# Last convolution of a four-layer network: swapped weight columns for every second row pair, stores of two rows in one run, whole images loaded

## Chip, cores and metric

The kernel runs on one core of one Trainium2 chip, in float32. The metric is device time in microseconds (us) of the whole program, from launch to the last output landed; lower is better. Times of several runs are given as their median. Besides these there is one execution taken by the hardware profiler, from which every duration below comes.

## What is computed

The input x has 8 images of 16 channels with 256 x 256 pixels. Four residual layers follow one another, each of the form x = x + f(group norm of x): a 3x3 convolution with capsule routing, a 3x3 convolution over B-spline and SiLU features, an attention over 16x16 patches, and last a convolution. Only the last one matters here. The reference writes it with Fourier transforms:

```python
def _L3_conv_ref(x, weight):
    B, Ci, H, W = x.shape
    k, p = (K_SIZE, PAD)
    w_pad = _circular_pad(weight, H, W, k, p)
    dL = jnp.asarray(np.outer(_diag_L(H, k), _diag_L(W, k)))
    Lw = jnp.fft.fft2(w_pad * dL)
    Kx = jnp.fft.ifft2(x, norm='ortho')
    z = jnp.einsum('oihw,bihw->bohw', Lw, Kx)
    y = jnp.fft.fft2(z, norm='ortho')
    return jnp.real(y).astype(x.dtype)
...
x = x + _L3_conv_ref(_gn(x), L3_conv_weight)
```

A product of Fourier transforms is a circular convolution, and the mask dL keeps all nine taps of the 3x3 kernel. So each output pixel is a sum over 16 channels and 3x3 neighbours, where rows and columns wrap around at the image's edges, plus the pixel itself (the residual). The group norm has 8 groups of two channels: it is a scale and a shift per image and group.

## The kernel before

The program runs the layers in turn (net_kernel, L1608). Layers 0, 1 and 2 keep their results in HBM scratch; layer 0's order of work comes from a planner with due times, layers 1 and 2 are loops written out by hand. Their code is not touched, except that layer 2 fetches the first image of layer 3 and that two constants grow.

How the last layer's input lies. Layer 2 (attend, L1402) makes one channel of one image at a time and stores it to self.x3[b], a scratch of [8, 16, 16, 2, 258] (r, c, h, k, w). With g = 2h + k, the entry (r, c, g) is image row 8g + r of channel c, with one wrapped pixel added on each side. Read with (r c) as partition, an image is a [128, 32 x 258] tile: partition (r, c) holds 32 rows, eight apart. The first 32 partitions need a 33rd row, the image's first, for the wrap.

The convolution as matmuls. Four blocks of 32 partitions hold two image rows (r = 2k, 2k + 1) of 16 channels each. A matmul contracts one such block (K = 32) with a 32 x 32 weight block, whose columns are (output channel, ro), ro being one of two output rows; its moving operand is two rows g, g + 1 of 256 pixels, so N = 512. An output row pair needs four input rows, that is two blocks (q = 0, 1), and three column shifts dw: 6 matmuls. products (L1519) runs for one s (a quarter image), one q: 3 shifts x 4 row pairs j x 4 column groups c, 48 matmuls. [...] Output row 1 + 8g + 2j + ro of channel o ends in PSUM partition 32c + 2o + ro, at j and g. In before, g = 8s + 2c, so that a quarter s covers 64 rows and the four column groups 16 rows each.

The scale of the norm is multiplied into the weights, and the identity of the residual is added (weights, L1507, one VectorE instruction of 192 columns per image); the shift becomes a bias that the eviction adds.

Eviction and stores. finish (L1535) evicts the two PSUM tiles of a quarter with two instructions of 128 x 1024 into y3, a [128, 2, 4, 256] tile with five buffers: even quarters on ScalarE (L1545), odd ones on VectorE (L1543). Then SP stores it with eight DMAs (L1553), one per column group c and per ro. A partition holds rows of one parity, so each row of 256 pixels is a run of 1 KB by itself, 16 channels x 8 rows per DMA, 128 KB; row 256 wraps to row 0 with a DMA of its own. An image takes 33 of them.

Loads. The tile pt[0] of layer 2 (early2, L1291) is free while the last image runs; there first3 (L1390) loads 24 of the 32 rows of image 0 on SP's queue, when channel 6 is reached. The other 9 rows (x3r) and a copy of rows 23 to 25 (x3e[...]) come at the start of layer 3, on SP. All other images come in halves of 17 (or 16 + 1) rows, tile x3s with five buffers, on POOL's queue (fetch, L1497): five halves are asked for at once, then one more at each half as a buffer comes free, which is when TensorE has read the half that was in it.

The order within layer 3 is that of the code (tc.manual_schedule, L1578): per image b and half (s = 0 and 2), four PSUM tiles[...]; q = 0 for both quarters, each followed by two small copies ("seen", L1594); then q = 1 for both, each followed by finish. The statistics of the last image's norm ("g3b") run as small steps between the halves. [...]

The constants and weights that grow: ident3 is part of a constant block loaded after layer 0 (net_kernel, L1612; constants, L302), w3 is loaded in early3 (L1303).

Of the kernel before, what the change touches and what calls it, by code (L numbers as in the profile page):

```python
# [10 lines left out]
F32 = mybir.dt.float32  # L11
# [7 lines left out]
P = 128  # L19
WP = W + 2  # L20
# [86 lines left out]
def _ident3():  # L107

    a = np.zeros((4, 2, C, 3, 2, C, 2), np.float32)
    for c in range(C):  # L110
        for ro in range(2):
            a[:, 1 - ro, c, 1, ro, c, ro] = 1.0
    return a.reshape(P, 3 * 2 * 32)
# [16 lines left out]
def _layout(w0, bw, sw, sc, bias, wq, bq, wk, bk, wv, bv, w3):  # L130
# [37 lines left out]
    l3 = l3.reshape(P, 3 * 2 * 32)  # L168
# [110 lines left out]
class _Net:  # L279
# [950 lines left out]
    def stats3_steps(self, pool, name, bank):  # L1230
# [31 lines left out]
        def sums():  # L1262

            for q in range(4):
                at = slice(32 * q, 32 * q + 32)
                for k in range(6):
                    nc.tensor.matmul(
                        z()[at, :8], self.w3[at, k // 2, k % 2], nm[at], start=k == 0, stop=k == 5
                    )
# [21 lines left out]
    def early2(self, pool):  # L1291

        self.w2 = {
            name: pool.tile(shape, F32, name=f"w2_{name}")
            for name, shape in dict(qk=[P, 2, 512], v=[P, 2, 256], bqk=[P, 512], b2v=[P, 2]).items()
        }
        self.pt = [pool.tile([P, 2, C, 8, 32], F32, name="pt0")]
        self.emb0 = pool.tile([P, 2, 256], F32, name="emb0")
        self.mv2 = pool.tile([P, 2, 8], F32, name="mv2")
        self.nc.vector.memset(self.mv2, 0.0)  # L1300
        self.small = pool

    def early3(self, pool):  # L1303

        self.st3 = pool.tile([P, P, 6], F32, name="st3"), pool.tile([P, 2, P], F32, name="mv3")
        self.nc.vector.memset(self.st3[1], 0.0)
        self.w3 = pool.tile([P, 3, 2, 32], F32, name="w3")
        self.nc.sync.dma_start(out=self.w3.rearrange("p d t m -> p (d t m)"), in_=self.d["l3"])
        self.small = pool
# [80 lines left out]
    def first3(self, b):  # L1390

        xs = self.pt[0].rearrange("p h c r f -> p (h c r f)")[:, : 24 * WP].rearrange("p (g w) -> p g w", w=WP)
        self.fetch3(b, 0, 24, xs)
        self.x3s = xs
# [67 lines left out]
    def fetch3(self, b, g, n, xs):  # L1462

        rows = self.x3[b].rearrange("r c h k w -> (r c) (h k w)")
        at = xs.rearrange("p g w -> p (g w)")
        for k in range(g, g + n, 8):
            m = min(8, g + n - k)
            if k < 32:
                self.nc.sync.dma_start(
                    out=at[:, (k - g) * WP : (k - g + m) * WP], in_=rows[:, k * WP : (k + m) * WP]  # L1470
                )
            else:
                self.nc.sync.dma_start(out=at[0:32, (k - g) * WP : (k - g + 1) * WP], in_=rows[0:32, 0:WP])

    def layer3(self, images=range(B)):
# [6 lines left out]
        with ExitStack() as st:  # L1482
# [14 lines left out]
            def fetch(n):  # L1497
                xs = io.tile([P, 17, WP], F32, name="x3s", bufs=5)
                rows = self.x3[images[n // 2]].rearrange("r c h k w -> (r c) (h k) w")
                if n % 2:  # L1500
                    nc.gpsimd.dma_start(out=xs[:, :16], in_=rows[:, 16:])
                    nc.gpsimd.dma_start(out=xs[:32, 16], in_=rows[:32, 0])
                else:
                    nc.gpsimd.dma_start(out=xs, in_=rows[:, :17])
                return lambda k, g: xs[32 * k : 32 * k + 32, g - n % 2 * 16 : g - n % 2 * 16 + 2]

            def weights(b):  # L1507
                ws = io.tile([P, 3, 2, 32], F32, name="ws3")
                nc.vector.scalar_tensor_tensor(
                    ws.rearrange("p d t m -> p (d t m)"),  # L1510
                    self.w3.rearrange("p d t m -> p (d t m)"),
                    stat[b][0][:, 1, b : b + 1],
                    self.k["ident3"],
                    ALU.mult,
                    ALU.add,
                )
                return ws

            def products(s, q, ws, xs, ps):  # L1519

                for dw in range(3):
                    for j in range(4):
                        k = (j + q) % 4
                        for c in range(4):
                            g = 8 * s + 2 * c + (j + q) // 4
                            nc.tensor.matmul(  # L1526
                                ps[j // 2][32 * c : 32 * c + 32, j % 2].rearrange("p (g w) -> p g w", w=W),
                                ws[32 * k : 32 * k + 32, dw, q],
                                xs(k, g)[:, :, dw : dw + W],
# [5 lines left out]
            def finish(b, s, ps):  # L1535

                y = io.tile([P, 2, 4, W], F32, name="y3", bufs=5)
                bias = stat[b][1][:, b : b + 1]
                for k in range(2):
                    src = ps[k].rearrange("p j (g w) -> p g j w", w=W)  # L1540
                    to = y[:, :, 2 * k : 2 * k + 2]
                    if s % 2:
                        nc.vector.tensor_scalar(to, src, bias, None, ALU.add)  # L1543
                    else:
                        nc.scalar.activation(to, src, AF.Identity, bias=bias)  # L1545
                for c in range(4):
                    for ro in range(2):
                        row = 64 * s + 16 * c + 1 + ro
                        n = 8 if row + 14 < H else 7
                        yc = y[32 * c : 32 * c + 32].rearrange("(o r) g j w -> r o (g j) w", r=2)[ro]  # L1550
                        for first, m, at in ((0, n, row),) if n == 8 else ((0, 7, row), (7, 1, 0)):
                            to = self.out[b, 0, at]
                            nc.sync.dma_start(  # L1553
                                out=bass.AP(tensor=to.tensor, offset=to.offset, ap=[[H * W, C], [2 * W, m], [1, W]]),
                                in_=yc[:, first : first + m],
                            )

            images = list(images)
            rest = io.tile([P, 9, WP], F32, name="x3r", bufs=1)
            self.fetch3(images[0], 24, 9, rest)  # L1560
            edge = io.tile([P, 3, WP], F32, name="x3e", bufs=1)
            nc.sync.dma_start(
                out=edge, in_=self.x3[images[0]].rearrange("r c h k w -> (r c) (h k) w")[:, 23:26]
            )

            def first(k, g):
                part = slice(32 * k, 32 * k + 32)
                if g + 2 <= 24:
                    return self.x3s[part, g : g + 2]
                return edge[part, g - 23 : g - 21] if g == 23 else rest[part, g - 24 : g - 22]  # L1570

            seen = [io.tile([P, 2, 2], F32, name=f"seen{k}", bufs=1) for k in range(2)]
            halves = 2 * len(images)
            xs = {0: first, 1: first}
# [3 lines left out]
            with tc.manual_schedule():  # L1578
                for n in range(2, min(7, halves)):
                    xs[n] = fetch(n)  # L1580
                for n, b in enumerate(images):
                    for s in (0, 2):
                        i = 2 * n + s // 2
                        if 7 <= i + 4 < halves:
                            xs[i + 4] = fetch(i + 4)
                        ps = [[psum.tile([P, 2, 512], F32, name="p3") for _ in range(2)] for _ in range(2)]
                        for q in range(2):
                            for k in range(2):
                                products(s + k, q, ws, xs[i], ps[k])
                                if q:  # L1590
                                    finish(b, s + k, ps[k])
                                else:
                                    for h in range(2):
                                        (nc.vector.tensor_copy if k else nc.scalar.copy)(  # L1594
                                            seen[k][:, h], ps[k][h][:, :, 0]
                                        )
                        if todo:
                            todo.pop(0)[2]()
# [75 lines left out]
```

## Time and profile before

| what | value |
|---|---|
| median of 3 runs | 6721.79 us (6716.23 to 6725.06) |
| profiled execution, its time | 6718.79 us |
| profiled execution, its span | 6716.9 us |
| layer 3, first to last matmul | 6447.4 to 6697.9 us, 250.5 us |
| from the last eviction's end (6700.2) to the span's end | 16.7 us |
| stores issued at L1553 | 264 |
| TensorE busy over the whole span | 91% |
| mean granted TensorE clock | 0.985 |

The span is the time from the first to the last instruction of the profiled execution; its own time is 1.9 us longer, and lies 3.0 us below the median. Engines: PE is TensorE, PEld its weight load, DVE VectorE, ACT ScalarE, POOL GpSimd, SP the queue that issues most DMAs. DMA queue q1 holds what SP issues, q0 what POOL issues, q8 the instruction blocks. A float32 matmul appears as two instructions. "Issue" as a releaser means that the engine waited for nothing that the profile shows.

Layer 3 is 3.7% of the span. The rest, layers 0 to 2, is the same code in both kernels.

### The profile page before, as it was taken

To read this page: it belongs to the slowest core of one execution; us is meant where nothing else is said; L and a number is where in the kernel's file an instruction comes from. 1 tells how busy PE (TensorE), PEld (TensorE's weight loads), DVE (VectorE), ACT (ScalarE), POOL (GpSimd) and SP (SyncE) were. 2 spreads that over 40 slices of the span, in tenths; PEclk is the share of its full clock that TensorE was granted. 3 is DMA by queue.
4 is the path that set the end of the run, shared out by engine and by line. 5 is a ranking of instruction groups with operands and counts; after the bars stand their busy time and mean duration, and the time that the engine had idled before them with its cause. 6 is when DMAs were issued, how large, how long until landed. Compare 5 with 4: busy or idle time off the path is not lost. (4 is left out here: it accounts for less than half of the span.)

```text
span 6716.9 us, 111531 instructions
## 1 busy us (share of the span) xinstructions
PE 6114.0 (91%) x46024; PEld 2774.9 (41%) x46024; DVE 5400.4 (80%) x6374; ACT 2737.3 (41%) x3898; POOL 3230.2 (48%) x2098
## 2 busy tenths in 40 slices
PE   3899899899989999898897799999999999999998
PEld 1333333333333333333333344444444466666655
DVE  5799999999999999999998899999999633333321
ACT  1333333333333333333332688888888421111211
POOL 0566666666666666666667444434334211111100
PEclk9999999999999999999998899999999999999999
DMA  6233333333333333333332555555556633334257
GB/s 260 61 87 90 92 91 93 90 88 91 91 90 91 89 88 88 88 88 88 88 88 61 171 176 177 176 176 178 176 175 177 178 86 87 80 93 106 74 190 220
DMA packets 392784, 801.99 MB, mean 119 GB/s; under 512 B 57282, under 2 KB 222178, under 8 KB 354770
## 3 DMA queue, kind: packets, MB, share of 16 engines
q1 hardware_dynamic: 356242, 730.29, 37.7%
q10 hardware_dynamic: 33792, 33.82, 1.5%
q0 software_dynamic: 2240, 30.75, 1.2%
q8 instruction: 361, 5.91, 0.4%
q14 instruction: 149, 1.22, 0.1%
HBM read 584.00 MB, written 210.77 MB: 118 GB/s over the span
## 5 line engine op out<-in xcount | busy, mean ns | idle before, releaser
L745 POOL TENSOR_TENSOR dd<-dd 128x1024 f32<-128x1024 f32 x512 | 1214.0, 2371 | 617.1 <-DVE dd L736 597.1
L1001 PE MATMUL ps<-bases,tw 128*32 128x512 f32 (+1 forms) x13824 | 1361.4, 546 | 17.1 <-POOL bases L970 7.0
L736 DVE SCALAR_TENSOR_TENSOR dd<-rb,v 128x1024 f32<-128x1024 f32 (+1 forms) x1024 | 1066.9, 1083 | 99.0 <-PE rb L725 92.5
L970 POOL TENSOR_TENSOR bases<-e,a 128x1024 f32<-128x1024 f32 (+1 forms) x264 | 621.4, 2376 | 929.0 <-DVE e L968 928.7
L624 DVE TENSOR_TENSOR pr<-v,fb 128x2048 f32<-128x2048 f32 (+1 forms) x512 | 1011.6, 2017 | 24.1 <-PE pl L634 12.7
L518 PE MATMUL cv<-kt,w 128*128 128x512 f32 x2048 | 999.4, 610 | 27.9 <-DVE dd L736 21.5
L527 ACT COPY v<-cv 128x1024 f32<-128x1024 f32 x512 | 517.1, 1010 | 1152.9 <-PE cv L522 1152.9
L1001 PEld LDWEIGHTS ps<-bases,tw 128*32 128x32 f32 x13824 | 594.4, 109 | 805.6 <-issue 485.4
L745 POOL TENSOR_TENSOR s<-s,dd 128x512 f32<-128x512 f32 x512 | 670.8, 1310 | 35.0
L725 PE MATMUL rb<-rs,ct_fold 32*128 32x512 f32 x3584 | 610.2, 651 | 71.4 <-ACT rs L707 67.9
L745 POOL TENSOR_TENSOR s<-v,dd 128x512 f32<-128x512 f32 x256 | 330.7, 1292 | 660.2 <-DVE dd L736 660.2
L634 PE MATMUL pl<-pr,ct_fold 128*32 128x512 f32 x3584 | 534.3, 608 | 120.1 <-DVE pr L624 120.1
L522 PE MATMUL cv<-kt,w 64*128 64x512 f32 x2048 | 578.7, 641 | 0.0
L518 PEld LDWEIGHTS cv<-kt,w 128*128 128x128 f32 x2048 | 353.7, 190 | 524.0 <-issue 298.9
L1426 ACT ACTIVATE vt<-pv,w_b2v 128x128 f32<-128x128 f32 x512 | 146.2, 368 | 842.4 <-PE pv L1422 842.4
L1415 PE MATMUL pqk<-w_qk,t 128*128 128x512 f32 x1024 | 482.7, 594 | 4.6 <-POOL t L1409 4.6
L1447 DVE TENSOR_TENSOR y<-po,res 128x512 f32<-128x512 f32 x128 | 88.5, 691 | 487.3 <-PE po L1442 487.3
L978 DVE SCALAR_TENSOR_TENSOR bases<-xr,xm,bases 128x1024 f32<-128x1024 f32 (+1 forms) x264 | 447.6, 1734 | 0.3 <-POOL bases L970 0.3
L1409 POOL TENSOR_TENSOR t<-t,emb 128x512 f32<-128x512 f32 x128 | 162.3, 1268 | 511.0 <-DVE t L1405 500.3
L955 ACT ACTIVATE sq<-a 128x1024 f32<-128x1024 f32 (+1 forms) x264 | 263.8, 999 | 229.5 <-DVE a L947 228.7
L725 PEld LDWEIGHTS rb<-rs,ct_fold 32*128 32x128 f32 x3584 | 173.3, 186 | 416.4 <-issue 221.1
L937 ACT ACTIVATE d<-xr,bd,sd 128x1024 f32<-128x1024 f32 (+1 forms) x264 | 319.0, 1208 | 15.8 <-DMA xr<-x1p 15.8
(264 smaller groups left out, 8386.1 us busy)
## 6 DMA issues: line engine op xcount, KB each, us to landing
kt<-d SPq DMA_DIRECT2D x256, 516.0 KB
xr<-x1p SPq DMA_DIRECT2D x120, 1024.0 KB
d<-dn ACTq DMA_DIRECT2D x64, 516.0 KB
x<-y SPq DMA_DIRECT2D x128, 258.0 KB
xs<-in_x_dram SPq DMA_DIRECT2D x16, 2048.0 KB
xs<-in_x_dram SPq DMA_DIRECT2D x64, 512.0 KB
res<-in_x_dram SPq DMA_DIRECT2D x64, 512.0 KB
x<-s SPq DMA_DIRECT2D x128, 256.0 KB
```

The lines of the kernel that those rows point to most:

```text
L518: nc.tensor.matmul(ps()[:, n], w[:, 0, j, :], t[:, a : a + 2, 0:W], start=True, stop=False)
L522: nc.tensor.matmul(ps()[:, n], w[at, 1, j, :], t[at, a : a + 2, 2 - n : 2 - n + W], start=False, stop=True)
L527: nc.scalar.copy(v[h]()[:, 4 * g : 4 * g + 4, j * W : j * W + W], ps().rearrange("p n (a w) -> p (n a) w", w=W),)
L624: nc.vector.tensor_tensor(pr()[:, :n].rearrange("p n (r w) -> p n r w", w=W), v[h]()[:, 4 * g : 4 * g + n].rearrange("p n (r w) -> p n r w ...
L634: nc.tensor.matmul(pl()[at : at + 32], sel[:, g, h, :], pr()[:, t, :], start=h == 0 and g == 0, stop=h == 1 and (g == 1 or t == 3),)
L725: nc.tensor.matmul(r()[:, n], spread[at, g, h, :], rs()[at], start=True, stop=True)
L736: nc.vector.scalar_tensor_tensor(dd()[:, :n], r()[:, :n], 1.0 / B, v[h]()[:, a : a + n], ALU.subtract, ALU.mult)
L745: op("POOL", us, lambda: nc.gpsimd.tensor_tensor(out[0](), a[0](), b[0](), ALU.add), a[1] + b[1], out[1])
L970: nc.gpsimd.tensor_tensor(ring[n % 3][:, 0, p : p + m, 1 : 1 + W], rows(e), rows(a), ALU.subtract)
L978: nc.vector.scalar_tensor_tensor(r, rows(part[1]), xm[:, b : b + 1], v, ALU.is_gt, ALU.mult)
L1001: nc.tensor.matmul(out if k is None else out[:, k], lhs, rhs, start=start, stop=stop, skip_group_check=True)
L1415: nc.tensor.matmul(ps, t[:, n, k * P : (k + 1) * P], wqk[:, n, :], start=n == 0, stop=n == 1)
```

## The change

- The weight columns exist twice: as before, and with the last axis (ro) turned round (_turned). products takes the turned ones for odd j. So for odd row pairs the two output rows change places among the partitions: partition (o, 0) then holds rows 0, 3, 4, 7, 8, ... of its part and (o, 1) rows 1, 2, 5, 6, ...: two neighbouring rows of a channel lie side by side in one partition.
- g is 8c + 2s instead of 8s + 2c: a column group covers 64 rows of the image, and the two quarters of a half lie side by side, so that a half gives each column group 32 rows on end.
- y3 holds a half image, [128, 2, 2, 4, 256], with four buffers; evict is the first part of finish, and store issues all DMAs of a half after both evictions: per column group one of 8 and one of 7 runs of two rows (2 KB), and one with the two single rows left at the ends. An image takes 25 DMAs.
- Images are loaded whole: image 0 into pt[0]'s tile, made 33 rows long (x30), during layer 2; two more into x3s (two buffers) at the start of layer 3; image n + 2 into the tile of image n - 1 when the second half of image n is reached in the code, for n of 1 to 5. fetch3 issues two DMAs of 16 rows and one of the 33rd row. x3r and x3e are gone.
- ident3, w3 and the scaled weights have 384 columns instead of 192.

```diff
-    return a.reshape(P, 3 * 2 * 32)
+    return _turned(a)
+
+
+def _turned(a):
+
+    return np.concatenate([a.reshape(P, 3 * 2 * 32), a[..., ::-1].reshape(P, 3 * 2 * 32)], 1)
...
-        self.pt = [pool.tile([P, 2, C, 8, 32], F32, name="pt0")]
+        self.x30 = pool.tile([P, 33 * WP], F32, name="pt0")
+        self.pt = [self.x30[:, : C * 512].rearrange("p (h c r f) -> p h c r f", h=2, c=C, r=8)]
...
-        xs = self.pt[0].rearrange("p h c r f -> p (h c r f)")[:, : 24 * WP].rearrange("p (g w) -> p g w", w=WP)
-        self.fetch3(b, 0, 24, xs)
-        self.x3s = xs
+        self.fetch3(self.nc.sync, b, self.x30.rearrange("p (g w) -> p g w", w=WP))
...
+        for k in range(0, 32 * WP, 16 * WP):
+            engine.dma_start(out=at[:, k : k + 16 * WP], in_=rows[:, k : k + 16 * WP])
+        engine.dma_start(out=at[:32, 32 * WP :], in_=rows[:32, :WP])
...
-                            g = 8 * s + 2 * c + (j + q) // 4
+                            g = 8 * c + 2 * s + (j + q) // 4
...
-                                ws[32 * k : 32 * k + 32, dw, q],
-                                xs(k, g)[:, :, dw : dw + W],
+                                ws[32 * k : 32 * k + 32, j % 2, dw, q],
+                                xs[32 * k : 32 * k + 32, g : g + 2, dw : dw + W],
...
+            def store(b, s, y):
+
+                y = y.rearrange("(c o r) s g j w -> r o c (s g j) w", c=4, r=2)
+
+                def put(row, ap, src):
+                    to = self.out[b, 0, row]
+                    nc.sync.dma_start(out=bass.AP(tensor=to.tensor, offset=to.offset, ap=[[H * W, C], *ap]), in_=src)
+
+                row = 16 * s + 1
                 for c in range(4):
...
+                    for r, n in ((1, 8), (0, 7)):
+                        put(
+                            row + 64 * c + 3 - 2 * r,
+                            [[4 * W, n], [1, 2 * W]],
+                            y[r, :, c, 1 - r : 1 - r + 2 * n].rearrange("o (m t) w -> o m (t w)", t=2),
+                        )
+                    if row + 64 * c + 31 < H:
+                        put(row + 64 * c, [[31 * W, 2], [1, W]], y[0, :, c, 0:16:15])
+                    else:
+                        put(row + 64 * c, [[W, 1], [1, W]], y[0, :, c, 0:1])
+                        put(0, [[W, 1], [1, W]], y[0, :, c, 15:16])
...
-                for n in range(2, min(7, halves)):
-                    xs[n] = fetch(n)
+                for b in images[1:3]:
+                    xs.append(fetch(b, io.tile([P, 33, WP], F32, name="x3s")))
                 for n, b in enumerate(images):
                     for s in (0, 2):
-                        i = 2 * n + s // 2
-                        if 7 <= i + 4 < halves:
-                            xs[i + 4] = fetch(i + 4)
+                        y = io.tile([P, 2, 2, 4, W], F32, name="y3", bufs=4)
+                        if s and n and n + 2 < len(images):
+                            xs.append(fetch(images[n + 2], xs[n - 1]))
...
+                                    evict(b, s + k, ps[k], y)
...
+                        store(b, s, y)
```

## The prediction

> **What bounds the kernel now.** The change touches only the last stage, so I asked for busy time stretch by stretch there, one stretch per half image (16 halves, 6447.4 to 6697.9 us), then for what ends TensorE's idle time, then for the DMA queues.
>
> Busy time by half (after the PE, PEld, DVE, ACT and POOL columns: granted clock, DMA share, GB/s):
>
> ```profile
> 6485.30:6498.50 13.20, 13.20 (x387) 8.99 (x387) 1.70 (x5) 2.44 (x4) 0.00 (x0) 1.00 0.76 174
> 6498.50:6514.70 16.20, 14.66 (x392) 8.36 (x393) 4.32 (x10) 3.72 (x5) 1.04 (x2) 1.00 0.84 255
> 6514.70:6532.40 17.70, 15.72 (x387) 9.12 (x386) 3.77 (x12) 4.24 (x7) 0.55 (x1) 0.90 0.86 261
> ...
> 6646.80:6659.50 12.70, 12.70 (x395) 9.53 (x373) 2.60 (x5) 2.44 (x4) 0.00 (x0) 1.00 0.81 185
> ```
>
> A half without a load beside it (POOL 0.00) takes 12.7 to 13.2 us; one in which POOL has issued a load takes 15.5 to 17.7. The floor is 16 x 12.8 = 205 us; the stage takes 250.5. So 45 us are lost: 12.3 in halves 0 and 1, 0.4 in half 2, 33.1 in the nine halves 3 to 11 (148.3 - 9 x 12.8), nothing in the last four.
>
> TensorE's order of time there (start, length, line, count, [idle before <- releaser]):
>
> ```profile
> 6498.51 9.03 PE L1526 MATMUL p<-x3s,ws 32*32 32x512 f32 x244
> 6509.08 5.35 PE L1526 MATMUL p<-x3s,ws 32*32 32x512 f32 x140 [1.53 <-issue]
> ...
> 6556.88 13.28 PE L1526 MATMUL p<-x3s,ws 32*32 32x512 f32 x383 [1.64 <-issue]
> 6571.80 13.93 PE L1526 MATMUL p<-x3s,ws 32*32 32x512 f32 x384 [1.64 <-issue]
> ```
>
> No engine and no buffer releases these gaps ("issue"), and 140 + 242, 383, 384 matmuls lie between them: multiples of 128, that is of 256 instructions with the weight loads. The DMA queues in the first of these halves, 6502 to 6506 us and 6506 to 6510 us (packets, MB, share of 16 engines):
>
> ```profile
> q0 software_dynamic: 84, 1.39, 100.2%
> q1 hardware_dynamic: 47, 0.03, 2.5%
> ```
>
> ```profile
> q1 hardware_dynamic: 1112, 1.01, 73.2%
> q0 software_dynamic: 48, 0.03, 2.8%
> q8 instruction: 1, 0.02, 1.5%
> ```
>
> While a load (q0) runs it owns the engines; stores (q1) stand still, and no instruction block (q8, 16 KB) comes. Cut into 1 us windows, q8 packets lie 4 to 5 us apart in halves without loads, and 7 to 8 us apart once per load (6547, 6554; 6562, 6569; 6578, 6585). In the opening burst, with loads back to back for 28 us, they lie 6 to 7 apart. So what bounds the stage is TensorE's instruction stream, delayed by loads, not matmuls and not store bandwidth.
>
> The end, 6700 to 6717 us:
>
> ```profile
> q1 hardware_dynamic: 3280, 2.97, 76.3%
> ...
> out_dram<-y SPq DMA_DIRECT2D x20, 128.0 KB
> ```
>
> SP still issues 20 stores after the last eviction (6700.2): it ends at 6714.25, so 0.70 us per 128 KB, and the span ends 2.65 later. Behind a load, queued stores reach 0.37 MB in 1 us; here they make 0.19 to 0.20. So the tail is paced by SP's issues.
>
> [...] in the opening burst q0 and q1 indeed run one packet against one (21 and 21 in the window at 6475), and 17 KB against 1 KB is why stores crawl. [...] So longer rows buy little by themselves.
>
> **The change, part by part**, against the profiled execution (span 6716.9, 6718.79 with what surrounds it; 3.0 under the median 6721.79).
>
> Stores. 33 issues an image become 25 (264 to 200), mostly 2 KB rows and 224 or 256 KB. In mid-stage they have cover: 12.5 x 0.70 = 8.8 us of SP per 12.8 us half. Stores start only when both evictions of a half are done, some 6.4 us later for the first; four half-image buffers instead of five quarters absorb it. Behind a waiting store SP queues only further stores, for which nothing but a y buffer waits. The waits of DVE and ACT for y buffers (35.2 + 41.6 us) go, for nothing: no TensorE gap is released by an eviction (0.7 us in all). If cover fails, SP's queue grows and the tail with it. A 256 KB issue I price from the x3 store of L1458, 258 KB: median 0.579 us, against 0.601 for L1553; size costs no issue time. Bounds: 0.5 to 1.0 us. Tail: 13 issues after the last eviction, 8 at 0.70 and 5 small ones at 0.5 = 8.1, + 0.3 to start, + 2.65 = 11.1, against 16.7 now: -5.6 (bounds -3 and -7; 2.1 MB at 0.37 MB/us needs 5.7, so DMA does not bind).
>
> Opening burst. Image 0 comes whole during layer 2: 4.2 MB instead of 3.1 at 6355 on SP, with the x3 stores queued behind. 1.1 MB at 0.43 MB/us is 2.6 us of DMA, TensorE is busy for 50.00 of 50 us from 6350 on, and y2's three buffers give three channels of 8.77 us: nothing, and if that cover failed, 2.6. Then POOL loads images 1 and 2: 8.5 MB instead of 10.6 on POOL plus 1.4 on SP. At 0.42 MB/us that is 20 us rather than 28. In the 28 us, six blocks took 37.9 us, 12.3 / 6 = 2.05 lost each; in 20 us I count four, plus 0.7 for the drain after: 8.9 lost for 12.3, -3.4 (bounds -1, -6). The 3.6 us for which the first weights wait on the last x3 store (6443.2 to 6446.9) are not touched.
>
> Steady loads. Nine half loads (2.1 to 2.2 MB, 6.6 us each) become five whole ones (4.2 MB), each two large DMAs back to back and a 32-partition row, some 13 us with stores (now 2 KB against each 16.5 KB) taking turns. Each starts when the image two places back has been read; its own use is an image later (over 25 us), so data are not late. POOL has nothing queued behind that wait. A block interval caught by a load's start is about 7.3 us, one inside a burst 6.4 (opening), one in the drain about 5; normal is 4.28. Sum: 7.3 + 6.4 + 5 - 3 x 4.28 = 5.9 per image, 6.0 with clock dips (0.90 in three of nine halves now). 5 x 6.0 = 30.0 for 33.1: -3.1. The trace has no two-load burst under steady stores. Bounds: one caught interval per image (3.2) or three that each cost the nine halves' mean of 3.68, dips included (11.0). I take 6.0, because it lies between the two observed cases.
>
> Weights. The product of weights and scale has 384 columns for 192 (0.41 us): about 0.6; seven of eight lie under matmuls, the first stands before the first matmul: +0.2 (uncovered all eight, 1.6). The constants and w3 grow by 98 KB each: the first is issued near the layer 0 to 1 turn: 0 to 0.3, taken 0.2. Matmul count, eviction sizes and padding copies stay; addressing g as 8c + 2s moves nothing. The edge and rest fetches leave SP.
>
> Sum: -5.6 - 3.4 - 3.1 + 0.4 = -11.7. From the profiled 6718.8 that is 6707.1; from the median, 6710.1, which I give as 6710. Next limit: still block fetches, then 205 us of matmuls.
>
> **Rivals.** (A) A whole-image load catches only one block[...]; lost per image 3.2, 16 in all for 33.1: -17.1, with -8.6 elsewhere -25.7, 6696. For it: each load now catches essentially one. Against: the opening burst delayed every block. (B) Slower: the longer burst, with fatter store rows taking turns, delays three blocks per image at 3.68 each: 55.2 for 33.1, +22.1, less 8.6 elsewhere = +13.5, 6735; it decides from (33.1 + 8.6) / 5 = 8.3 us lost per image. For it: three of nine halves show the clock at 0.90, losing 4.4 to 4.9. Against: halves without dips lose about 3.2. (C) The 2 KB rows are cut to 1 KB again by the descriptors: SP still issues less often, so the tail differs by at most 2 us; inside the main case.
>
> **How the numbers follow.** Main case 0.58 (own range 6703 to 6718), A 0.27, B 0.15. About 0.2% (13.4 us) is what a measurement can tell from no change; the main case lies just inside and passes it in four of ten. Faster 0.58 x 0.4 + 0.27 = 0.50; slower: half of B, 0.08; within 0.42. Range 6694 to 6725: it leaves out about a third of A (0.09) and three quarters of B (0.11).
>
> **What would show it.** Tail after the last eviction near 11 us; images 1 to 5 at about 25.6 + 6.0 = 31.6 us each and the last two at 25.6; q8 intervals of 6 to 8 only under q0; the opening two halves near 34.5. I am wrong if images 1 to 5 need 29 us or 36, if gaps appear without q0, or if SP is still busy with older stores when the last eviction ends.

## The result, and the profile after

| | before | after |
|---|---|---|
| median | 6723.09 us (6716.22 to 6732.54, 12 runs) | 6714.61 us (6711.94 to 6719.18, 12 runs) |
| profiled execution, its time | 6718.79 us | 6716.81 us |
| profiled execution, its span | 6716.9 us | 6714.9 us |
| layer 3, first to last matmul | 250.5 us | 248.8 us |
| last eviction's end to the span's end | 16.7 us | 13.4 us |

The ratio of the two kernels' times is 0.9988, with a 95% interval of 0.9979 to 0.9997: 8.5 us faster (2 to 14), clear of no change, but less than the 0.2% that the prediction took for the least that a measurement can tell. The two profiles differ by 2.0 us only, because layers 0 to 2 ended 3.2 us later in the one of after (layer 3's first matmul at 6450.6 instead of 6447.4). That is well inside the scatter: in the profiles of the experiments below, which all load image 0 whole during layer 2 as after does, this point lies between 6447.1 and 6456.4. From that matmul to the span's end it is 269.5 us before and 264.3 after: 5.2 us less. That is what the profile can explain; where the other 3 us of the median's 8.5 lie is not shown.

Where the 5.2 us come from: 1.7 from the matmuls (250.5 to 248.8), 0.2 from the last eviction, 3.3 from what follows it. Stretch by stretch, the busy times of after, for the halves of images 1 and 2 and one half of image 7, without a load (columns as before: PE, PEld, DVE, ACT, POOL, then granted clock, DMA share, GB/s):

```profile
6484.40:6502.60 18.20, 14.88 (x388) 8.59 (x388) 3.34 (x7) 2.44 (x4) 1.08 (x3) 0.97 0.89 327
6502.60:6519.60 17.00, 16.76 (x388) 10.14 (x388) 3.91 (x10) 3.72 (x5) 0.00 (x0) 0.83 0.69 153
6519.60:6538.50 18.90, 15.38 (x388) 8.12 (x387) 4.02 (x12) 4.13 (x7) 1.59 (x3) 0.93 0.88 319
6538.50:6554.40 15.90, 15.90 (x404) 9.74 (x404) 3.63 (x9) 2.44 (x4) 0.00 (x0) 0.87 0.71 159
...
6673.50:6686.40 12.90, 12.90 (x413) 9.38 (x411) 3.00 (x5) 2.44 (x4) 0.00 (x0) 1.00 0.77 173
```

In these two images a half with a load beside it (POOL over 0) takes 18 to 19 us, of which TensorE is busy for 15; the half after it has almost no idle time (0.24 us at most), but takes 16 to 17, at a granted clock of 0.83 and 0.87. The last two images, without loads, are back at 13 us a half. The eight images take 33.9, 35.2, 34.7, 30.5, 32.0, 30.2, 26.3 and 25.9 us. The low clock is not spread over the half. These are a part of one such half, the rest of it, and the whole stage:

```profile
6501.60:6508.40 6.80, 6.80 (x109) 2.97 (x102) 2.35 (x6) 0.00 (x0) 0.00 (x0) 0.50 0.76 174
6508.40:6519.60 11.20, 10.96 (x305) 7.38 (x287) 1.65 (x4) 3.72 (x5) 0.00 (x0) 1.00 0.63 139
...
6450.60:6699.40 248.80, 227.26 (x6204) 134.77 (x6204) 49.54 (x89) 41.91 (x68) 11.02 (x21) 0.95 0.83 249
```

For 6.8 us the clock stands at 0.50, and 109 matmuls run where the pace of the next stretch would make about 190. The stage has five such stretches (from its start, 6501.6, 6535.8, 6593.8 and 6631.3 on; 3.3, 6.8, 6.8, 3.4 and 3.4 us of it), so by this estimate half of 23.7 us, 12 us, are lost to the clock. The 44 us above the floor (248.8 - 205) are thus 21.5 us in which TensorE is idle, 12 at half clock, and some 10 in slower matmuls and in the steps of the last norm. In before they were 22.4 us idle and about 8 at a low clock (0.97 over the stage).

The gaps are of the kind shown before, the longest of them 2.8 us instead of 2.5 (TensorE's order of time; in brackets the idle time before and its releaser):

```profile
6493.74 4.47 PE L1519 MATMUL p<-x3s,ws 32*32 32x512 f32 x128 [0.48 <-issue]
6501.05 1.42 PE L1519 MATMUL p<-x3s,ws 32*32 32x512 f32 x9 [2.83 <-issue]
...
6529.23 4.47 PE L1519 MATMUL p<-x3s,ws 32*32 32x512 f32 x128 [0.95 <-issue]
6536.26 1.95 PE L1519 MATMUL p<-x3s,ws 32*32 32x512 f32 x13 [2.56 <-issue]
```

No engine and no buffer releases them, 128 matmuls with their weight loads, 256 instructions, lie between two, and a packet of q8 comes 2.2 to 2.4 us before each of the four ends (at 6491.5, 6498.7, 6527.0 and 6533.9). From 6451 to 6700 us q8 moves 49 packets and 0.80 MB, 16 KB each, and PE and PEld run 2 x 6204 instructions, 253 to a packet. So I read the gaps as waits for the next instruction block. Images 1 to 5 have two each of over 0.4 us, and 18.0 us of idle time in all; in before it was 17.7.

The tail, 6701 to 6717 us, in the DMA queues (packets; MB; share of 16 engines over the window):

```profile
DMA packets 1298, 2.10 MB, mean 131 GB/s; under 512 B 209, under 2 KB 338, under 8 KB 1298
q1 hardware_dynamic: 1298, 2.10, 59.8%
...
out_dram<-y SPq DMA_DIRECT2D x4, 256.0 KB
out_dram<-y SPq DMA_DIRECT2D x4, 224.0 KB
```

960 of the 1298 packets are not under 2 KB: the runs of two rows travel as such, which settles rival C (they are not cut to 1 KB). But their 2.10 MB take 10.5 us from the first packet to the last, 0.20 MB/us, the pace of the 1 KB runs of before (2.93 MB in 14.9 us). What fell is the amount left at the last eviction, to the 2.10 MB of one half image.

And the waits in layer 3 that end on something else than the engine's own input (us in total, times, longest):

```profile
ACT y L1537 <- DMA out_dram<-y: 28.9, 5, 5.8
PE p L1519 <- issue: 21.4, 16, 2.8
DVE y L1535 <- DMA out_dram<-y: 12.5, 1, 12.5
```

The evictions still wait for y buffers, 41.4 us in total for 76.8 before; TensorE waits for none of them.

### The profile page after: what moved, and what is told of

Same layout as the page of the kernel before. It is cut to its first block, busy times and chain, and to the rows that moved or that the text cites. A ratio compares the mean times of both kernels' runs of the same rounds, so it can differ in the third digit from the quotient of the medians.

```text
span 6714.9 us, 111421 instructions
## 1 busy us (share of the span) xinstructions
PE 6114.2 (91%) x46024; PEld 2770.4 (41%) x46024; DVE 5401.2 (80%) x6374; ACT 2737.7 (41%) x3898; POOL 3231.7 (48%) x2098
## 5 line engine op out<-in xcount | busy, mean ns | idle before, releaser
L523 PE MATMUL cv<-kt,w 128*128 128x512 f32 x2048 | 1000.1, 610 | 28.2 <-DVE dd L741 21.4
```

The costliest lines, as they stand in the source:

```text
L523: nc.tensor.matmul(ps()[:, n], w[:, 0, j, :], t[:, a : a + 2, 0:W], start=True, stop=False)
```

## The experiments

The theory after the result: in layer 3, instruction blocks come late while loads fill the DMA engines (matmuls 248.8 us against 205 without loss), and the tail is set by the rate of the stores. Rivals: stores or y buffers hold TensorE; the tail is set by SP's issues; the run length of stores or of loads sets the loss. "Matmuls" is the time from layer 3's first to its last matmul, "tail" that from the last eviction's end to the span's end, both from the profile. In after they are 248.8 and 13.4. All edits are to the kernel after.

### Loads left out, stores left out

```diff
-                for b in images[1:3]:
-                    xs.append(fetch(b, io.tile([P, 33, WP], F32, name="x3s")))
...
-                                products(s + k, q, ws, xs[n], ps[k])
+                                products(s + k, q, ws, xs[0], ps[k])
```

(and the later fetches too); in the second kernel

```diff
-                        store(b, s, y)
+                        if n + 1 == len(images) and s:
+                            store(b, s, y)
```

> The changed kernel without the loads of layer 3: every image is convolved from image 0's tile, so images 1 to 7 of the output are left out as such. Theory (loads delay the instruction blocks of TensorE): layer 3's matmuls take about 16 x 12.8 = 205 us instead of 248.8, no gaps with releaser 'issue' over 0.5 us, granted clock 1.00, whole time about 44 us less. Rival (store traffic, or evictions that wait for a y buffer, stall TensorE): most of the 44 us stays, since all stores are still there.

> The changed kernel with all loads, but only the very last half image is stored, the other 15 halves of the output are left out. Theory (loads delay the blocks): images 0 to 5 keep gaps of 1 to 3 us at multiples of 128 matmuls; layer 3's matmuls lose at least 25 of the 44 us, the rest at most being the stores' share of the load time. Rival (stores stall TensorE): under 10 us lost. The tail after the last eviction stays near 13 us, since the last half's stores are the same.

In the first kernel all eight images are computed from image 0's pixels; in the second only the last half image reaches the output. Each ran once. Without loads: matmuls 213.1 us, no gap above 0.4 us, tail 13.4, time 6678.31 us. The stores went on as before, ScalarE and VectorE waited 47 us for y buffers, and that cost TensorE nothing:

```profile
ACT y L1537 <- DMA out_dram<-y: 29.2, 5, 5.8
DVE y L1535 <- DMA out_dram<-y: 17.8, 3, 5.9
```

The images 3 to 6 take 25.3 to 25.5 us there, with all stores under way: stores without loads cost TensorE nothing. The 8 us over 205 lie mostly in images 0 to 2 (28 to 29 us each), beside the steps of the last norm; 1.7 of them are a stretch of 3.4 us at half clock.

Without stores: matmuls 233.7 us, gaps at multiples of 128 matmuls as before, tail 14.4. So of the 35.7 us that go with the loads (248.8 - 213.1), 20.6 stay when the stores are taken out, and 15.1 come only with loads and stores together. TensorE's idle time is 21.5 us in after, 14.1 without stores and 0.4 without loads; what the low clock costs is 12, 7 and 1.7 us. The first half of the theory holds for the waits. The low clock comes with the loads, too: in after each of its stretches begins in a wait of 1.8 us or more, or within 0.6 us of its end. But a wait of 2.0 us (to 6468.3) brought none, so that the waits cause it is likely, and not shown.

### Runs of 1 KB in the stores

```diff
+                    for r in range(2):
+                        n = 16 if row + 64 * c + r + 30 < H else 15
+                        put(row + 64 * c + r, [[2 * W, n], [1, W]], y[r, :, c, 0:n])
...
-                                ws[32 * k : 32 * k + 32, j % 2, dw, q],
+                                ws[32 * k : 32 * k + 32, 0, dw, q],
```

> The changed kernel with the weight columns not swapped, so that the rows are stored as runs of 1 KB; 8 DMAs of 256 KB per half (one more in the last), all else as after. First theory (a store's pace is set by the 16 of 128 partitions in one 32-partition block that it reads, not by its runs): stores alone still move 0.19 to 0.20 MB per us, tail 13 us, time within 0.1% of the changed kernel, a ratio to the kernel before of 0.998 to 1.000. Rival (longer runs were worth something): stores alone at 0.17 or less, tail 15 us or more, 3 to 10 us slower than the changed kernel.

The weight columns are not turned, so each row is a run by itself, and a half image goes in 8 DMAs of 256 KB; the rest is the kernel after. 6727.65 us (13 runs), ratio to before 1.0005 (0.9997 to 1.0014), where after has 0.9988 (0.9979 to 0.9997): the swapped columns are worth 11 us by the ratios and 13 by the medians within this design, against my "within 0.1%", and as the two intervals meet, the size is loose. The tail doesn't show it: 13.6 us, and the stores alone still move 0.19 to 0.20 MB/us. What can be seen is under the loads. Two windows of 2 us, each inside the load of an image; of the kernel with 1 KB runs,

```profile
q0 software_dynamic: 51, 0.83, 96.3%
q1 hardware_dynamic: 49, 0.05, 7.0%
```

and of the kernel after:

```profile
q0 software_dynamic: 49, 0.79, 92.5%
q1 hardware_dynamic: 43, 0.09, 11.1%
```

In these windows the queues share the engines run by run: about as many runs of one pass as of the other (51 and 49, 49 and 43). With runs of 2 KB the stores moved 0.09 MB instead of 0.05. With 1 KB more is left over when the load ends: VectorE's wait for y buffers grows from 12.5 to 44.5 us in total. Matmuls take 254.3 us, 5.5 more, and TensorE's waits for blocks 24.4 us instead of 21.4. It waits for no eviction, so by what way shorter runs slow it is not shown; another 2.7 us of the difference of the two profiles lie before layer 3.

### Whole-image loads alone

```diff
-                            g = 8 * c + 2 * s + (j + q) // 4
+                            g = 8 * s + 2 * c + (j + q) // 4
...
-                        store(b, s, y)
+                                    finish(b, s + k, ps[k])
```

> Only the loads of the change: whole images, image 0 in layer 2; weight columns not swapped, evictions and stores per quarter image as in the kernel before (33 DMAs of 128 KB per image, five buffers). If the loads' new shape is a wash in the steady part and saves 3 to 4 us in the opening, as measured after, this is -2 us (0 to -5) with the old tail of 16 to 17 us. If the half-image stores mattered beyond the tail (fewer issues, more buffers), images 1 to 5 take longer than in the changed kernel (32.5 us on average) by over 1 us each, and the time is above that of the kernel before.

Quarter images are stored with 1 KB runs as before, only the loads are those of after: 6717.16 us (13 runs), ratio 0.9989 (0.9981 to 0.9998), matmuls 248.5, tail 15.1. By its ratio it can't be told from the kernel after (0.9988), so the loads' part of the change carries most of the gain, and with quarters stored as they come the 1 KB runs do no harm. The kernel with 1 KB runs above, with the same loads, but half images stored (and g = 8c + 2s), is 10.5 us slower: storing by half image costs what the longer runs bring back, and what can be seen of both together is the shorter tail. One difference goes beyond the loads: with g = 8s + 2c the two halves of a tile are read out half an image apart, so the two large DMAs of a load start apart, too.

### Shorter runs in the loads

```diff
-        for k in range(0, 32 * WP, 16 * WP):
-            engine.dma_start(out=at[:, k : k + 16 * WP], in_=rows[:, k : k + 16 * WP])
+        for k in range(0, 32 * WP, 4 * WP):
+            engine.dma_start(out=at[:, k : k + 4 * WP], in_=rows[:, k : k + 4 * WP])
```

> The changed kernel with each whole-image load cut into eight DMAs of 4 rows (runs of 4.1 KB per partition instead of 16.5), same bytes, same moment. Theory (an instruction block waits in its engine's line behind load runs of 0.7 us each): runs of a quarter of the length cut the wait, blocks come at 5 us or less under loads, layer 3's matmuls take 248.8 minus 10 to 25 us, whole time 10 to 25 us under the changed kernel. Rival (only the bytes of a burst matter): within 4 us of the changed kernel.

> As with 4 rows, but 16 DMAs of 2 rows (runs of 2.06 KB), near the stores' 2 KB. Theory (wait behind load runs): stores then share the engines evenly with the load and blocks are hardly delayed; matmuls of layer 3 in 210 to 230 us, whole time 20 to 35 us under the changed kernel. Rival (bytes): within 4 us. Second rival (POOL's issues, 16 at 0.53 us, or the cost per run slow the load until data come late): gaps released by the load, 5 us or more slower.

If a block had to wait behind one 16.5 KB run on each engine, runs of 4 or 2 KB should free it. With 4 rows: 6710.66 us (9 runs), ratio 0.998 (0.9971 to 0.999), matmuls 242.1. With 2 rows: 6712.67 us (21 runs), ratio 0.998 (0.9974 to 0.9987), matmuls 247.1. Both intervals overlap with that of the kernel after. In the opening burst blocks still came 6 to 7 us apart with 4 rows, 5 to 7 with 2. TensorE's start of layer 3 with 4 rows:

```profile
6459.24 4.49 PE L1519 MATMUL p<-pt,ws 32*32 32x512 f32 x128 [0.66 <-issue]
6465.46 1.04 PE L1519 MATMUL p<-pt,ws 32*32 32x512 f32 x2 [1.73 <-issue]
```

TensorE's idle time is 17.7 and 17.0 us, for 21.5 with runs of 16.5 KB. So the length of a load's run sets a small part of the delay at most. This theory, which asked for 10 us or more, falls.

### Loads in paced pieces

```diff
+                                    if k and more:
+                                        nc.gpsimd.tensor_copy(rung, seen[k][:, 0, 0:1])
+                                        self.piece3(images[n + 1], xs[n + 1], s + 1)
```

(and the same after each half's evictions, waiting for y; piece3 loads 8 rows). In the second kernel, the last half's stores too:

```diff
-                    nc.sync.dma_start(out=bass.AP(...), in_=src)
+                    (nc.scalar if b == images[-1] and s and c > 1 else nc.sync).dma_start(out=bass.AP(...), in_=src)
```

> Edit to the kernel after: every image is asked for one image ahead in four pieces of 8 rows (1.06 MB, some 2.5 us each), and POOL issues a piece only when a copy or an eviction of the running image has been reached (a one-element copy on POOL waits for it), so that the pieces lie about 6.4 us apart, in the opening too. The arithmetic and the bytes are those of the kernel after. Theory 1 (an instruction block is late because it is asked for inside a long stretch in which loads fill all 16 engines; a stretch of 2.5 us delays it by at most that[...]): layer 3's matmuls near 220 us, between 213 and 232, in place of 248.8, no gap over 1.5 us, time near 6688. Theory 2 (a block pays for the bytes that are loaded and stored beside it, however they are spread, or the fetch is slow whenever any load is under way): matmuls within 5 us of 248.8, the loss spread evenly over seven images, time within 6 us of the kernel after. In between (some 235): both play.

> Edit to the kernel with paced pieces: in the last half image alone, when no load is left, the stores of the column groups 2 and 3 are issued by ScalarE on its own queue and those of groups 0 and 1 by SP. Theory (the tail is set by stores that read one 32-partition block at a time, 0.20 MB/us; two queues that read both halves of the partitions move 0.31): the 2.1 MB need 6.7 us in place of 10.5, so that the tail after the last eviction is about 10.5 us in place of 13.4, and the time 3 us below the run with paced pieces alone. Rival (the tail is set by what follows the last store, or by SP's issues): tail 13 to 13.5 us, time the same as with paced pieces alone, since SP's issues are halved but the last landing stays.

6745.68 us (7 runs), ratio 1.0026 (1.0015 to 1.0038); matmuls 273.0 us. Both theories missed, each in the wrong direction: the loss grew by 24 us. Images 0 and 1 and the whole stage, with granted clock, DMA share and GB/s at the end of each line:

```profile
6456.40:6493.50 37.10, 33.41 (x777) 18.97 (x777) 6.53 (x12) 4.79 (x8) 3.14 (x8) 0.87 0.55 174
6493.50:6530.90 37.40, 31.91 (x773) 17.82 (x772) 5.78 (x14) 6.27 (x9) 3.37 (x9) 0.90 0.71 229
...
6456.40:6729.40 273.00, 242.44 (x6204) 139.67 (x6204) 49.12 (x89) 42.02 (x68) 24.59 (x63) 0.91 0.74 227
```

The DMA engines are idle 29 to 45% of the time in these two images, and yet TensorE is idle for 30.6 us of the stage, for 21.5 in after. Its waits for blocks are 26.7 us (21.4), 16 of over 0.4 us (12), so many pieces catch somewhat more blocks than few long stretches; 3.5 us more are waits for data that came late, since an image was asked for just one image ahead. Half of the 24 us is the clock, 0.91 for 0.95 over the stage: by the estimate used above it costs about 24 us instead of 12. A small part of the start shows a block beside a piece. 6457 to 6462 us holds the first piece and nothing else, no store:

```profile
q0 software_dynamic: 144, 1.06, 61.0%
```

and 6462 to 6463:

```profile
q8 instruction: 1, 0.02, 6.0%
```

This block comes 1.5 us after the piece, and TensorE did not have to wait for it. At the second piece (6466 to 6469) the next block came as the piece ended, at 6469.6, and here TensorE waited 0.9 us, to 6471.9. So a block can be late beside a single piece, alone on the engines; two cases don't show that the piece held it.

The second kernel was to split the last half's stores. It measured 6754.49 us (5 runs), but its SP queue stood still for 24.0 us around the last image's end (6702.1 to 6726.1), waiting for a store to land, so that SP still had some 4.2 MB to move after the last eviction, and the tail of 29.8 us does not answer the question as it was put. What that wait was for I did not settle. One thing can be read: from 6728 to 6732 both queues ran and moved 0.78 MB, 0.20 MB/us, no more than one alone. By the order of its issues SP was then at column groups 2 and 3 of an earlier half image, the same partitions as ScalarE. The next two kernels test this.

### Two queues for the stores

```diff
-                    nc.sync.dma_start(out=bass.AP(...), in_=src)
+                    (nc.sync if c < 2 else nc.scalar).dma_start(out=bass.AP(...), in_=src)
```

> The changed kernel with the stores of column groups 0 and 1 (partitions 0 to 63) issued by SP and those of 2 and 3 (partitions 64 to 127) by ScalarE's queue. Theory[...]: the two queues together move 0.33 MB per us or more, the tail after the last eviction falls from 13.4 to 8 to 9.5 us, whole time 4 to 10 us under the changed kernel. Rival (HBM writes or the engines themselves end at 0.20 MB per us when nothing else runs): tail 12 to 14 us.

> As the one before, but SP takes column groups 0 and 2, ScalarE's queue 1 and 3, so that at a time both read partitions 0 to 63 (groups 0 and 1), then both 64 to 127. Theory[...]: still about 0.20 MB per us, tail 12 to 13.5 us. Rival (one queue cannot feed the engines faster, two can): the tail falls as with the other split, to 8 to 10 us.

In the second kernel ScalarE's queue takes the odd column groups instead of the last two. As kernels both are slow, 6816.9 us (ratio 1.0135, 1.0121 to 1.0148) and 6831.9 us, for a reason of their own: ScalarE's stores meet a load (q0 moves at 0.3 to 0.4 MB/us from 6489 to 6501), ScalarE is held in issuing them, and its small "seen" copies, for which TensorE waits (99.0 us in 15 waits in the first), come late. From ScalarE's order of time in the first,

```profile
6489.51 16.80 ACTq L1545 DMA_DIRECT2D out_dram<-y  x7
6506.35 0.22 ACT L1586 COPY seen<-p 128x2 f32<-128x2 f32 x2 [20.47 <-DMA out_dram<-y]
```

But the tail answers its question. 5 us of it (6812.6 to 6817.6, from where both run) with groups 0, 1 on SP and 2, 3 on ScalarE:

```profile
DMA packets 949, 1.59 MB, mean 317 GB/s; under 512 B 136, under 2 KB 214, under 8 KB 949
q10 hardware_dynamic: 483, 0.82, 53.3%
q1 hardware_dynamic: 466, 0.77, 44.1%
```

5 us of it (6819 to 6824) with groups 0, 2 and 1, 3:

```profile
DMA packets 624, 1.02 MB, mean 203 GB/s; under 512 B 96, under 2 KB 160, under 8 KB 624
q10 hardware_dynamic: 320, 0.52, 50.1%
q1 hardware_dynamic: 304, 0.49, 42.9%
```

Two queues move 0.32 MB/us and leave a tail of 10.6 us if they read partitions 0 to 63 and 64 to 127 at the same time; they move 0.20 and leave 13.2 us, as one queue does, if they read neighbouring blocks. The second kernel ran once; both splits give each queue the same issues. So neither SP's issues nor the length of a run sets the tail, but which partitions are read at once. Measured are 0.20 MB/us for one 32-partition block or two of the same half, and 0.32 for one of each half: more than one half alone, though not twice as much. What limits a half, no view shows.

### Loads on another queue

```diff
-                self.fetch3(nc.gpsimd, b, xs)
+                self.fetch3(nc.scalar, b, xs)
```

in the second kernel nc.sync, with the loads of images 3 to 7 in two parts, each behind a half image's stores:

```diff
+                        if n and n + 2 < len(images):
+                            tile_in = fetch(images[n + 2], xs[n - 1], s // 2)
```

> Edit to the kernel after: ScalarE issues the loads of layer 3 on its own hardware queue in place of POOL on the software queue q0; the same DMAs at the same places of the order, everything else unchanged. Paced pieces have shown that neither the length of a load nor the distance between loads sets the loss, so the queue itself or the bytes remain. Theory S (an instruction block is delayed by the software queue[...]): with loads on a hardware queue the gaps are mostly gone, layer 3's matmuls at 213 to 228 us in place of 248.8, time some 20 to 30 us below the kernel after. Theory B (any load from memory beside stores delays the block, whichever queue carries it): matmuls within 5 us of 248.8, block intervals of 6 to 8 us beside q10 as beside q0; the time within 6 us of the kernel after, or later by what ScalarE loses when its issues of loads block it (it has five loads of three DMAs to issue while stores are under way; at 2.4 us each that is up to 36 us on ScalarE, partly hidden).

> Edit to the kernel after: SP issues the loads of layer 3 on the queue of the stores, the first two images at the start of the layer and every later image in two parts of 16 rows, each behind the stores of a half image; POOL issues none. One queue then carries everything in layer 3 except instruction blocks, and loads and stores come one after the other instead of side by side. Theory S (the software queue delays the block): matmuls at 213 to 228 us if the single queue keeps up; it has 8.4 MB to move per image, 4.2 in at 0.42 and 4.2 out at 0.20 to 0.37 MB/us, that is 21 to 31 us for 25.6 us of matmuls, so that a growing backlog can show as waits of the evictions for y, and a tail of up to 20 us. Theory T (a block waits its turn among the other queues, and one queue fewer gives it a turn sooner): block intervals beside loads fall to about 5 us whichever kind of queue, matmuls 215 to 230. Theory B (any load delays a block): matmuls within 6 us of 248.8 with the gaps inside the load parts.

Loads on ScalarE's queue: 6713.91 us (21 runs), ratio 0.9989 (0.9983 to 0.9996), matmuls 241.9 and tail 17.5 us. On SP's: 6714.27 us (21 runs), ratio 0.9987 (0.998 to 0.9993), matmuls 245.9, tail 13.5. Both times are within 1 us of the kernel after, where theory S wanted some 20 to 30 less, and theory T matmuls of 215 to 230. TensorE with loads on ScalarE's queue, during the load of an image:

```profile
6555.04 4.48 PE L1519 MATMUL p<-pt,ws 32*32 32x512 f32 x128 [0.26 <-issue]
6562.08 12.50 PE L1519 MATMUL p<-pt,ws 32*32 32x512 f32 x318 [2.56 <-issue]
...
6591.51 4.49 PE L1519 MATMUL p<-x3s,ws 32*32 32x512 f32 x128 [1.51 <-issue]
6597.72 2.88 PE L1519 MATMUL p<-x3s,ws 32*32 32x512 f32 x75 [1.72 <-issue]
```

So theory B stands: a load delays blocks whichever queue carries it, beside the stores or between them (with loads on SP's queue TensorE still waits 21.2 us with "issue" as releaser, for 21.4 in after). ScalarE's loads spare 7 us of matmuls in this one profile and lose 4 in the tail. Most of the 7 is the clock, which costs 5 us there instead of 12; the idle time is 19.2 us for 21.5.

None of the ten kernels that do all the work is clearly below the kernel after; the lowest median, with loads of 4 rows, has an interval that overlaps.

## Why the prediction was right or wrong

The forecast was 6710 us with a range of 6694 to 6725, the median is 6714.6; by 0.13% it lies within 0.2%, for which I gave 0.42 against 0.50 for more. That the median came so near is in part luck: profile against profile the steps bring 5.2 us for the 11.7 of the forecast, and the rest of the median's 8.5 belongs to no step. Step by step (for images 1 to 5 the loss of before is taken over all five, 33.5 us):

| step | predicted | measured |
|---|---|---|
| tail | -5.6 (11.1 left) | -3.3 (13.4 left) |
| opening, image 0 | -3.4 (8.9 lost) | -4.0 (8.3 lost) |
| images 1 to 5 | -3.1 (31.6 us each) | +1.1 (32.5 us each) |
| last two images | 0 | +1.0 |
| weights, constants | +0.4 | product 0.61 us for 0.41, and the first matmul waits 6.1 us for it instead of 5.9; the rest is within the scatter of layers 0 to 2 |

**The bound** was read rightly as far as the loads go. Taking them out removes 35.7 us and every gap over 0.4 us; the y buffers, with 47 us of waits left, cost nothing. But waits for instruction blocks are only half of the loss. The prediction put all 45 us of before on them, of which TensorE was idle for 22.4, and gave the clock 0.1 us a load.

**The tail** is a term that was mis-sized, by a wrong mechanism: "the tail is paced by SP's issues". In before the two could not be told apart. SP made 22 issues there, two smaller ones besides the 20 that I counted, so one came every 0.65 us and not 0.70; 0.60 of it is the issue, and 128 KB at 0.20 MB/us take 0.65 us as well. Stores of 256 KB with the same 1 KB runs part them. These are the nine issues of the last half in the kernel with 1 KB runs (shortest, median and longest in ns):

```profile
L1545 SPq DMA_DIRECT2D out_dram<-y x9: 578/1284/1351, 6709.7 to 6718.8; - x9
```

The first two take 0.6 us, five of the later ones about 1.3, which is the time of 256 KB at 0.20 MB/us: what sets the pace there is the transfer, and SP waits for it. The evidence I put against the DMA side, 0.37 MB/us behind a load, may have another state behind it, stores of several column groups queued together; that is not tested. The right sum is the bytes left over the rate of one block: before, 14.9 us for 2.93 MB and 1.8 to the end make 16.7; after, 1.3 to the first packet, 10.5 for 2.10 MB and 1.6 make 13.4. The stated bound (-3 to -7) held.

**The opening** was right: 8.3 us lost for 8.9.

**The steady loads** failed in sign, though inside their bounds (3.2 to 11.0 a load). The count of late blocks was good: the three intervals between q8 packets, put at 7.3 + 6.4 + 5 = 18.7 us, came to 18.4, 17.9, 16.9, 18.3 and 18.5 in images 1 to 5. The step that failed is the clock, the 0.1 us in "6.0 with clock dips". Images 1 and 2 ran for 6.8 us at half clock, images 4 and 5 for 3.4, which costs 3.4, 3.4, 1.7 and 1.7 us, 10 in all, for 5 in before. With the steps of the last norm, which run in images 0 to 2 of both kernels, this sets the 9.6 and 9.1 us lost in images 1 and 2 apart from the 4.9, 6.4 and 4.6 of images 3 to 5; the idle time does not differ (3.6 and 3.5 us, against 3.0, 4.5 and 3.4). One of the signs that I named failed with it, "q8 intervals of 6 to 8 only under q0": two of 8.1 and 8.8 us come right after the loads beside images 1 and 2, while TensorE runs at half clock.

Rival B's point of decision, 8.3 us lost per image, was passed in images 1 and 2, but not by its mechanism: no more blocks were late there than in the other three. The mean, 6.9, stayed below it. In which images the clock falls differs from profile to profile (with whole-image loads and quarter stores it cost images 1 and 2 nothing, images 3 and 5 3.4 and 1.7 us), so the +1.1 of one execution says little about the loads. Rival A (one block per load) did not come: no loaded image lost under 4.6, and each had two waits.

**"So longer rows buy little by themselves"** was wrong, from the right observation: I had noted that queues take turns run by run and that this is why stores crawl, but drew the conclusion only from stores running alone. Alone, 1 and 2 KB move equally fast (0.19 to 0.20 MB/us). Beside a load the share went by run length (0.05 and 0.09 MB in 2 us), and with half images stored the kernel with 1 KB runs is 11 to 13 us slower; with quarters it is not.

**What stays open** is why a block is held up: neither the run length of loads (but for a small part), nor the queue, nor the length of a stretch sets it. When a block was asked for, no view shows. Open, too, is what sets off the stretches at half clock, which in these single profiles cost 5 us (loads on ScalarE's queue), 12 (after) or 24 (paced pieces) and make differences of a few us between them hard to read. And 3 of the 8.5 us are not placed.

## What to carry to other kernels

The time of an issue on its queue may be waiting for bandwidth (here 0.6 us for 256 KB on an empty queue, 1.3 on a full one): divide the bytes by the rate seen before calling it an issue cost, and look at which partitions are read together (0.20 MB/us from one half of the partitions, 0.32 from both). Where instruction blocks come late beside loads (in after up to 8.8 us apart, 4 to 5 in halves without loads in before), count the stretches of loads and what they catch, and test by taking the loads out; spreading them may make it worse. Split a loss into idle time and time at a lowered clock before explaining it: here they were nearly two to one, and two images that looked as if more blocks were late had no more late than the others. Run length is worth judging beside the other queue's traffic, not on a quiet one.

## What the runs showed of the hardware that was not expected

- Stores from one block of 32 partitions moved 0.19 to 0.20 MB/us with runs of 1 KB and of 2 KB alike; two queues in different halves of the partitions moved 0.32, in the same half 0.20.
- A single load of 1.06 MB, alone on the engines, was followed by the instruction block at 6462.5 us and another at 6469.6; with 28 such pieces TensorE waited 26.7 us for blocks, with seven whole images 21.4.
- ScalarE was held 16.8 us in the issue of seven stores that lay beside a load.
- In the kernel after the granted clock stood at 0.50 for 3.4 or 6.8 us at a time, from within or just after a wait on, and by an estimate from these lengths cost about 12 us of the stage. A long wait is not needed for it: without loads a stretch of 3.4 us came 2 us after a wait of 0.37, and that half took 15.05 us, at a clock of 0.72 in its first 6 us.
